# Audio tower on one Trainium2 core: sending each token's 1 / deviation through DRAM instead of through transposes, and moving one DCT ahead of the first gate

## The chip, the core and the metric

The kernel runs on one core of a Trainium2 chip, in float32 throughout. The metric is the time of one execution on the device, in microseconds (us). The time before is the median of three runs: 1388.79 us (1387.68 to 1390.09). The profiled execution took 1388.02 us, and its profile spans 1386.3 us.

The core has five engines that run their own instruction streams in order and wait for each other by semaphores: TensorE (PE; its weight loads are listed apart as PEld), VectorE (DVE), ScalarE (ACT), GpSimd (POOL) and SyncE (SP), which issues most DMA transfers.

## What is computed

There are 64 audio streams of 80000 samples. Each is cut into 157 frames of 512 samples, and a 512-point DCT turns each frame into a token `h` of 512 numbers. One layer follows, with an attention over the stream and a routed expert. Cut to what matters:

```
h = frames @ DCT.T                                   # 64 x 157 x 512
x = (h - mean(h)) / sqrt(var(h) + 1e-5)              # per token
key, query = tanh(x @ Wk + bk) * pi, tanh(x @ Wq + bq) * pi
V = x @ Wv + bv
total = sum over 4 sets of weight * Re(cumsum(e^(i key) V) * e^(-i query))
gate = sigmoid(x @ Wg + bg)
total = gate * total + (1 - gate) * pos_contribution
h = h + x + total / norm @ Wo + bo
x2 = layernorm(h);  e = argmax(softmax(mean(x2) @ Wg_ffn + bg_ffn))   # one expert per stream
h = h + score * (x2 @ We[e] + be[e])
```

The division by the deviation is what the change is about. The mean is taken out of the weights once, at the start of the program, so only one factor per token, 1 / deviation (`rstd`), has to reach the tokens before they are projected.

## The kernel before, in words

The 64 streams go in 16 groups of 4 (`NG`, `GB`). A group has 4 x 160 = 640 token slots, held as five tiles of 128 tokens (0 to 3 and `TAIL`). They stand in the order of `SLOT`, so that the first half of the slots (320, `HN`) is tile 0, tile 1 and half of the tail, and the second half is the rest of the tail and tiles 2 and 3.

A group's frames arrive as `xT`, 128 partitions x 4 x 640: samples on partitions, tokens along the free dimension. `fold_once` and `fold_twice` (lines 115 to 132) make the DCT cheaper by adding and subtracting mirrored samples in place. After that `xT` is both the operand of the DCT and, since the DCT is worked into the projection weights, the operand of all projections.

`embed` (line 241) does the DCT of one tile on PE into a PSUM buffer. `embed_statistics` (line 257) finishes it on DVE, takes its mean and variance there (lines 224 and 226), and lets POOL make `rstd` (lines 228 and 229), the shift (231) and `rstd` + 1 (267). `embed_res` (line 271) then reads the PSUM buffer on ACT (line 281) and writes the first part of the residual, which frees the buffer.

Here tokens lie on partitions, so `rstd` is one number per partition. In `xT` tokens lie along the free dimension, and there the factor must be the same in all partitions. `scale_all` (line 288) brings it there: six PE transposes (line 298) of `rstd`, repeated along the free dimension, fill a PSUM buffer, and two DVE multiplications (line 304), one for each half, scale `xT` in place.

All PSUM comes from one pool of four buffers of two banks each (line 83), taken in rotation by `psum()` and `bank()`. A buffer is taken again when all readers of its former content are through.

The order of the instructions on each engine is that of the program text: the schedule is written out by hand. From group 1 on, a group goes through `project_and_values`, `gate`, `experts_and_embedding` (the experts of the group before, the embedding of the next) and `attention`.

In `attention(g)` (line 1055), after the reading of the memory, the output projection is done as seven products (`output_product`, line 624), in the order 1, 2, 6, 7, 4, 5, 3. Product 7 is the one to follow:

- On DVE, product 7 is added to `u` (line 642).
- On POOL, three additions then take `u` into three quarters of the residual (line 630), `r22`, `r21` and `r12` in this order. They use `nc.gpsimd`, except in the last group.
- `scale_all(g + 1)` follows at once (line 1079).
- Product 4 is added into `r21` on DVE (line 657), product 5 into `r22` (line 647), then come the statistics of tiles 2 and 3 (`statistics2`), and the additions of products 5 and 3 into `r12`.
- `normal2(2)` makes the normalized tile 2 on ACT (line 677), after POOL has made its factor and shift.

`project_and_values(g + 1)` (line 960) begins on PE with the transposes of the normalized tail (line 690), the projection of keys and queries (line 524, on the scaled `xT`), and the transposes of normalized tile 2.

In the first group there is no such steady order. `first_values` ends with the DCT of tile 0 of group 1; `first_gate` (line 923) computes the gate of group 0 in four parts (`gate_part`, PE at line 560, ACT at 568) and between them does the rest of group 1's embedding, the scores, the additions of `bo` on POOL (line 286), and sums of the weights (`weights`, DVE at line 98).

Of the kernel before, what the change touches and what calls it, by code (L numbers as in the profile page):

```python
# [22 lines left out]
P = 128  # L23
# [30 lines left out]
def audio_tower(ctx: ExitStack, tc: tile.TileContext, a, out):  # L54
# [26 lines left out]
    p2 = pool("p2", 2)  # L81
    small = pool("small", 8)
    ps_mm = pool("ps_mm", 4, space=bass.MemoryType.PSUM)

    def load(name, shape, src=None):
        t = const.tile(shape, F32, name=name, tag=name)
# [3 lines left out]
    def psum():  # L90

        return ps_mm.tile([P, 2, 512], F32, tag="mm", name="mm")
# [31 lines left out]
    def fold_twice(g, m):  # L124

        if g < NG:
            ft, even = half(S[g]["xT"], m), S[g].pop(("even", m))
            add(ft[:, 2], even[:, 0], even[:, 1])
            sub(ft[:, 3], even[:, 0], even[:, 1])
            for n in range(2):  # L130
                to, by = ft[:, n], ft[:, 1 - n]
                nc.vector.scalar_tensor_tensor(to, by, lift[:, n : n + 1], to, ALU.mult, ALU.add)
# [85 lines left out]
        sub(raw, raw, ps.unsqueeze(1).to_broadcast([P, C, n]))  # L218


    def statistics(h):

        st = small.tile([P, 6], F32, tag="st", name="st")
        nc.vector.bn_stats(st, h)
        mv = small.tile([P, 2], F32, tag="mv", name="mv")
        nc.vector.bn_aggr(mv, st)  # L226
        rstd = small.tile([P, 1], F32, tag="rstd", name="rstd")
        nc.gpsimd.tensor_scalar(rstd, mv[:, 1:2], EPS, None, ALU.add)  # L228
        nc.gpsimd.tensor_tensor(rstd, rstd, power, ALU.pow)  # L229
        shift = small.tile([P, 1], F32, tag="shift", name="shift")  # L230
        nc.gpsimd.tensor_scalar(shift, mv[:, 0:1], rstd, -1.0, ALU.mult, ALU.mult)  # L231
        return rstd, shift
# [24 lines left out]
    def embed_statistics(g, n):  # L257
        s = S[g]
        h, odd = s.pop(("h", n))
        by_r = h.rearrange("p (j r) -> p r j", r=4)  # L260
        sines = p2.tile([P, P + 1], F32, tag="sines", name="sines")
        nc.scalar.copy(sines, odd[:, 1, : P + 1])
        add(by_r[:, 1, :], odd[:, 0, :P], sines[:, :P])
        sub(by_r[:, 3, :], odd[:, 0, 1 : P + 1], sines[:, 1 : P + 1])
        rstd, shift = statistics(h)
        rstd1 = small.tile([P, 1], F32, tag="rstd1", name="rstd1")
        nc.gpsimd.tensor_scalar(rstd1, rstd, 1.0, None, ALU.add)  # L267
        s["rstd", n] = rstd
        s["st", n] = h, shift, rstd1
# [14 lines left out]
    def add_bo(g, n):  # L284
        r = S[g]["res"][n]
        nc.gpsimd.tensor_tensor(r, r, bo, ALU.add)  # L286

    def scale_all(g):

        s = S[g]  # L290
        ps = psum()
        lo = 0

        for n in (0, 1, TAIL, TAIL, 2, 3):
            rows = slice(0, P) if n != TAIL else slice(0, HT) if lo < HN - 1 else slice(HT, P)
            m, at = divmod(lo, HN)
            w = rows.stop - rows.start
            nc.tensor.transpose(  # L298
                ps[:, m, at : at + w], s["rstd", n][rows].to_broadcast([w, P]), ident[rows, rows]
            )  # L300
            lo += w
        for m in range(2):
            x = half(s["xT"], m)
            nc.vector.tensor_tensor(x, x, ps[:, m, :HN].unsqueeze(1).to_broadcast([P, C, HN]), ALU.mult)


    def quarters(w):
# [230 lines left out]
    def phasors(g, of=(0, 1)):  # L538
        u = S[g]["u"]
        for n, to in ((0, kf), (1, qf)):  # L540
            if n not in of:
                continue
            for k in range(2):
                rows = slice(2 * F * k + F * n, 2 * F * k + F * (n + 1))
                to_k = to.rearrange("p s b t -> p (s b t)")[:, HN * k : HN * (k + 1)]
                nc.scalar.activation(to_k[F : 2 * F], u[rows, 0], AF.Sin, scale=PI)
                nc.scalar.activation(to_k[:F], u[rows, 1], AF.Sin, bias=quarter[rows], scale=-PI)
# [299 lines left out]
    def first_values():  # L847

        consts = constants()
        warm(12)  # L850
        made = [psum(), psum()]
        of = [ps[:, b, :] for ps in made for b in range(2)]
        for k in range(2):
            through_dct(raw_v, k, of[k], stop=False)
        total = add_up(raw_v, D, "x2T")
        for k in range(2, C):
            through_dct(raw_v, k, of[k], stop=False)
        fold_once(0, 0, nc.vector)
        fold_twice(0, 0)
        for k in range(C):  # L860
            less_mean(total, k, of[k])
            if k % 2:
                nc.scalar.copy(wv[:, k - 1 : k + 1], made[k // 2])
        embed(0, 0)
        embed(0, 1)
        embed_statistics(0, 0)
        embed_statistics(0, 1)
        embed_res(0, 0)
        embed_res(0, 1)
        value(0, 0)  # L870
        ps = psum()
        mean_kq, new_kq = ps[:, 0, : 2 * F], ps[:, 1, : C * 2 * F].rearrange("p (c n) -> p c n", c=C)
        means(add_up(raw_kq, 2 * F, "sum2"), mean_kq)
        centre(raw_kq, mean_kq, 2 * F)
        fold_once(0, 1, nc.vector)
        fold_twice(0, 1)
        value(0, 1)
        for k in range(C):
            through_dct(raw_kq, k, new_kq[:, k])
        nc.scalar.copy(wkq, new_kq)  # L880
        keep_value(0, 0)
        embed(0, 2)
        embed(0, 3)
        keep_value(0, 1)
        embed_statistics(0, 2)
        embed_statistics(0, 3)
        embed_res(0, 2)
        embed_res(0, 3)
        total = add_up(raw_g, D, "x2T", nc.gpsimd)
        value(0, 2)  # L890
        embed(0, TAIL)
        embed_statistics(0, TAIL)
        embed_res(0, TAIL)
        keep_value(0, 2)
        next(consts)
        value(0, 3)
        mean_g = bank()
        means(total, mean_g)
        centre(raw_g, mean_g, D)
        value(0, TAIL)  # L900
        keep_value(0, 3)
        keep_value(0, TAIL)
        scale_all(0)
        made = [psum(), psum()]
        for k in range(C):
            through_dct(raw_g, k, made[k // 2][:, k % 2])
        nc.scalar.copy(wg[:, :2], made[0])
        fold_once(1, 0)
        fold_twice(1, 0)
        fold_once(1, 1)  # L910
        project(0)
        nc.scalar.copy(wg[:, 2:], made[1])
        fold_phases(0)
        embed(1, 0)
        embed_statistics(1, 0)
        next(consts)
        phasors(0, (0,))
        embed_res(1, 0)
        phasors(0, (1,))
        next(consts)  # L920
        next(consts)

    def first_gate():

        made = chain(weight_sums(wv, t_v), weight_sums(wo, t_o))

        def weights():
            next(made)
            next(made)

        gate_part(0, 0)
        weigh()
        fold_twice(1, 1)
        weights()
        embed(1, 1)
        embed_statistics(1, 1)
        embed_res(1, 1)
        add_bo(0, 0)
        weights()
        gate_part(0, 1)  # L940
        scores(0)
        embed(1, 2)
        embed_statistics(1, 2)
        embed_res(1, 2)
        add_bo(0, 1)
        weights()
        gate_part(0, 2)
        weights()
        for n in (3, TAIL):
            embed(1, n)  # L950
            embed_statistics(1, n)
        for n in (3, TAIL):
            embed_res(1, n)
        gate_part(0, 3)
        for n in (2, 3, TAIL):
            add_bo(0, n)
        load_half(2, 0)
        load_half(2, 1)

    def project_and_values(g):  # L960

# [59 lines left out]
    def experts_and_embedding(g):  # L1021

        new = g + 1

        def embedded(n):
            embed_statistics(new, n)
            embed_res(new, n)

        add_bias(g - 1, TAIL)
        expert(g - 1, TAIL)  # L1030
        for n in range(3):
            embed(new, n)
            embed_statistics(new, n)
        add_bias(g - 1, 0)
        for n in range(3):
            embed_res(new, n)
        add_bv(g, 0)
        load_half(g + 2, 0)
        load_half(g + 2, 1)
        expert(g - 1, 0)  # L1040
        add_bias(g - 1, 1)
        add_bv(g, 1)
        expert(g - 1, 1)
        embed(new, 3)
        embed(new, TAIL)
        embed_statistics(new, 3)
        embed_statistics(new, TAIL)
        embed_res(new, 3)
        embed_res(new, TAIL)
        add_bias(g - 1, 2)  # L1050
        expert(g - 1, 2)
        add_bias(g - 1, 3)
        expert(g - 1, 3)

# [199 lines left out]
```

## Time and profile before

| | busy, us | share of the span | instructions |
|---|---|---|---|
| PE | 1376.4 | 99% | 10656 |
| PEld | 914.5 | 66% | 10656 |
| DVE | 1030.7 | 74% | 2076 |
| ACT | 402.9 | 29% | 690 |
| POOL | 604.3 | 44% | 858 |

The DMA engines moved 119.70 MB at a mean of 86 GB/s. Of the transfers, the frames (640 KB each) take a median of 4.6 us from issue to landing, and the result's pieces of 64 KB a median of 1.7 us.

The lines of the timeline read: start and duration in us, engine, line of the kernel, operation, tiles out<-in, partitions x elements out<-in, how many instructions in a row; in brackets the idle time before, and what ended it. A group of instructions starts where its first one starts. `mm` is a PSUM buffer. A lower-case q behind an engine's name is its sequencer.

### The profile page before, as it was taken

The numbers are of one execution on the slowest core, as the hardware profiler recorded it, in microseconds if no ns is written. First come the engines' busy times: TensorE is split into PE (matmuls) and PEld (weight loads), VectorE is DVE, ScalarE is ACT, GpSimd is POOL, SyncE is SP. The second block draws the span as 40 slices with busy tenths as digits, with TensorE's granted clock in tenths as the row PEclk, the third lists the DMA queues.
The fourth block names the chain that finished last, engine by engine and source line by source line (L and its number), as shares of the span: only waits on it lengthen the run. The fifth ranks groups of instructions, "written<-read, shape, count | busy, mean of one in ns | idle before, by whom it ended". The sixth has DMA issues, their size and how long they took to land.

```text
span 1386.3 us, 26936 instructions
## 1 busy us (share of the span) xinstructions
PE 1376.4 (99%) x10656; PEld 914.5 (66%) x10656; DVE 1030.7 (74%) x2076; ACT 402.9 (29%) x690; POOL 604.3 (44%) x858
## 2 busy tenths in 40 slices
PE   9999999999999999999999999999999999999998
PEld 5577575766758667575675757667586675766762
DVE  5768686777868778686776868778687777867674
ACT  2414242141422314242142422314223142421410
POOL 2453544525544254533535445255433545345314
PEclk9999999999999999999999999999999999999999
DMA  6013205032140323205032040322303232040306
GB/s 224 1 40 129 76 5 186 17 130 77 59 140 9 137 70 129 77 1 181 25 130 77 19 171 16 130 77 85 115 7 137 69 130 76 1 147 22 130 8 197
DMA packets 47293, 119.70 MB, mean 86 GB/s; under 512 B 9265, under 2 KB 26305, under 8 KB 39233
## 3 DMA queue, kind: packets, MB, share of 16 engines
q0 software_dynamic: 11456, 72.10, 13.5%
q1 hardware_dynamic: 35212, 45.26, 11.1%
q8 instruction: 84, 1.38, 0.4%
q10 hardware_dynamic: 500, 0.64, 0.2%
q14 instruction: 41, 0.33, 0.1%
HBM read 97.39 MB, written 20.58 MB: 85 GB/s over the span
## 4 chain that ended last, share of the span: by engine, by line
PE 97%; DVE 1%; DMA 1%; ACT 1%; issue 0%; POOL 0%; SPq 0%; DVEq 0%; POOLq 0%
PE mm L372 27%; PE mm L817 20%; PE mm L579 17%; PE mm L614 9%; PE mm L237 9%; PE mm L252 3%; PE mm L690 3%; PE mm L524 3%; PE mm L254 2%; PE mm L598 1%; PE mm L298 1%; PE mm L198 1%; PE mm L560 1%; DMA t_v<-in_we,rows 0%; DMA wv<-in_wv 0%; PE mm L709 0%
## 5 line engine op out<-in xcount | busy, mean ns | idle before, releaser
L228 POOL TENSOR_SCALAR rstd<-mv 128x1 f32<-128x1 f32 x160 | 44.6, 279 | 515.8 <-DVE mv L226 505.9
L817 PE MATMUL mm<-we,x2T 128*32 128x512 f32 x2400 | 267.4, 594 | 0.0
L817 PEld LDWEIGHTS mm<-we,x2T 128*32 128x32 f32 x2400 | 73.2, 110 | 161.3 <-issue 157.1
L99 DVE TENSOR_TENSOR gT<-mm,gT 128x128 f32<-128x128 f32 (+1 forms) x135 | 87.0, 673 | 82.6 <-PE mm L579 81.1
L622 DVE TENSOR_TENSOR gT<-mm,gT 128x320 f32<-128x320 f32 x256 | 116.8, 487 | 27.3 <-PE mm L614 22.9
L614 PE MATMUL mm<-att,v 32*128 32x256 f32 (+3 forms) x2048 | 123.6, 359 | 0.0
L614 PEld LDWEIGHTS mm<-att,v 32*128 32x128 f32 x2048 | 105.0, 185 | 22.3 <-issue 11.8
L589 ACT ACTIVATE gT<-gT,hbg 128x320 f32<-128x320 f32 x120 | 59.6, 554 | 168.6 <-DVE gT L99 168.6
L229 POOL TENSOR_TENSOR rstd<-rstd,power 128x1 f32<-128x1 f32 x160 | 98.1, 613 | 13.3
L828 DVE SCALAR_TENSOR_TENSOR res<-mm,gate,res 128x512 f32<-128x512 f32 x64 | 48.1, 751 | 68.3 <-PE mm L817 66.8
L677 ACT ACTIVATE x<-res,shift,rstd 128x512 f32<-128x512 f32 x64 | 52.1, 815 | 142.6 <-DVE res L99 101.0
L771 POOL DMA_INDIRECT we<-in_we,rows x60 | 62.0, 1034 | 71.4 <-DVE rows L767 57.7
L372 PE MATMUL mm<-t_o,sum 128*128 128x256 f32 x384 | 88.3, 379 | 0.4 <-DVE sum L98 0.4
L121 POOL TENSOR_TENSOR xT<-xT 128x640 f32<-128x640 f32 x30 | 46.7, 1557 | 91.6 <-DVE even L99 84.7
L286 POOL TENSOR_TENSOR res<-res,bo 128x512 f32<-128x512 f32 x64 | 85.6, 1366 | 0.0
L99 DVE TENSOR_TENSOR v<-mm,v 128x512 f32<-128x512 f32 x105 | 70.8, 686 | 18.8 <-PE mm L372 18.4
L372 PE MATMUL mm<-t_v,sum 128*128 128x256 f32 x360 | 82.7, 379 | 0.0
L281 ACT ACTIVATE res<-mm,shift,rstd 128x512 f32<-128x512 f32 x64 | 49.8, 778 | 103.9 <-POOL rstd L267 80.8
L372 PEld LDWEIGHTS mm<-t_o,sum 128*128 128x128 f32 x384 | 71.9, 190 | 11.7 <-PE mm L372 0.8
L231 POOL TENSOR_SCALAR shift<-mv,rstd 128x1 f32<-128x1 f32 x160 | 70.7, 442 | 16.5
L99 DVE TENSOR_TENSOR res<-mm,res 128x512 f32<-128x512 f32 x96 | 65.2, 685 | 15.0 <-ACT u L633 11.8
L630 POOL TENSOR_TENSOR res<-res,u 128x512 f32<-128x512 f32 x45 | 56.1, 1275 | 42.1 <-DVE u L99 42.1
(199 smaller groups left out, 2797.8 us busy)
## 6 DMA issues: line engine op xcount, KB each, us to landing
xT<-in_frames SPq DMA_DIRECT2D x32, 640.0 KB, 4.6
out<-res SPq DMA_DIRECT2D x236, 64.0 KB, 1.7
out<-res_t SPq DMA_DIRECT2D x62, 32.0 KB, 1.6
out<-res_t SPq DMA_DIRECT2D x62, 26.0 KB
wv<-in_wv SPq DMA_DIRECT2D x2, 512.0 KB, 5.5
wg<-in_wg SPq DMA_DIRECT2D x1, 1024.0 KB
wo<-in_wo SPq DMA_DIRECT2D x1, 1024.0 KB
we<-in_we,rows POOLq DMA_INDIRECT x60, 7.8
```

What stands on the lines that cost most here:

```text
L99: add = lambda *x: nc.vector.tensor_tensor(*x, ALU.add)
L229: nc.gpsimd.tensor_tensor(rstd, rstd, power, ALU.pow)
L231: nc.gpsimd.tensor_scalar(shift, mv[:, 0:1], rstd, -1.0, ALU.mult, ALU.mult)
L237: nc.tensor.matmul(ps, tile_of(x[:, c], n), w[:, c, :], start=(c == 0), stop=(c == C - 1))
L286: nc.gpsimd.tensor_tensor(r, r, bo, ALU.add)
L372: nc.tensor.matmul(ps[:, b, :], lhs[:, c, P * b : P * (b + 1)], w[:, c, :], start=(c == 0), stop=(c == 1))
L579: nc.tensor.matmul(ps[:, o, :HN], w[:, c, o * P : (o + 1) * P], rhs[:, c], start=(c == 0), stop=(c == 1))
L589: nc.scalar.activation(to, to, AF.Tanh, bias=hbg[:, c : c + 1], scale=0.5)
L614: nc.tensor.matmul(to, s["v", n][q, c * P : (c + 1) * P], by, start=(n == 3), stop=(n == TAIL))
L622: nc.vector.tensor_tensor(th, r[:, :, n], th, op)
L771: nc.gpsimd.indirect_dma_start(out=ws[b][:, n * k : n * (k + 1)], out_offset=None, in_=of, in_offset=bass.IndirectOffsetOnAxis(ap=rows[:, ...
L817: nc.tensor.matmul(ps[Q * i : Q * (i + 1), :], s["x2T"][:, c, i, Q * n : Q * (n + 1)], s["ws"][i][:, c, :], start=(c == 0), stop=(c == C - 1),
```

## The change

It has two parts.

**From group 1 on, `rstd` goes through DRAM.** `embed_statistics` writes it into a column of a tile `deviations`, 128 x 5. When all five are made, `keep_deviations` stores the tile to a row of 640 numbers in DRAM, in token order, and `spread_deviations` loads this row into all 128 partitions of a tile `scale` in SBUF. Both are issued from SP. `scale` shares its two buffers with `even`, the intermediate result of the folding. `scale_all` then has only the two multiplications, whose second operand is now in SBUF and no longer in PSUM. Group 0 keeps the transposes. In the steady order the store stands after the statistics of the tail in `experts_and_embedding`, the load after the expert of tile 2.

**In the first group the order changes.** The DCT of tile 1 of group 1 goes on PE ahead of `share` and the first gate part, its statistics ahead of the query phasors, and its `embed_res` behind them. One pair of weight sums moves behind gate part 1, and the others follow later.

```
-        rstd, shift = statistics(h)
+        if g == 0:
+            to = None
+        else:
+            if n == 0:
+                s["deviations"] = p2.tile([P, NM], F32, tag="deviations", name="deviations")
+            to = s["deviations"][:, SLOT[n] : SLOT[n] + 1]
+        rstd, shift = statistics(h, to)
...
+    def keep_deviations(g):
+
+        S[g]["row"] = row = dram.tile([NM, P], F32, tag="row", name="row")
+        nc.sync.dma_start(out=row.rearrange("s p -> p s"), in_=S[g]["deviations"])
+
+    def spread_deviations(g):
+
+        s = S[g]
+        s["scale"] = scale = p2.tile([P, 2, HN], F32, tag="even", name="scale")
+        row = s.pop("row").rearrange("s p -> (s p)")
+        nc.sync.dma_start(out=scale.rearrange("p m t -> p (m t)"), in_=row.partition_broadcast(P))
...
-        ps = psum()
...
+        if g == 0:
+            scale = psum()
...
+        else:
+            scale = s.pop("scale")
         for m in range(2):
             x = half(s["xT"], m)
-            nc.vector.tensor_tensor(x, x, ps[:, m, :HN].unsqueeze(1).to_broadcast([P, C, HN]), ALU.mult)
+            nc.vector.tensor_tensor(x, x, scale[:, m, :HN].unsqueeze(1).to_broadcast([P, C, HN]), ALU.mult)
...
         embed_statistics(1, 0)
+        embed(1, 1)
         next(consts)
         phasors(0, (0,))
         embed_res(1, 0)
-        phasors(0, (1,))
         next(consts)
         next(consts)
+        embed_statistics(1, 1)
+        phasors(0, (1,))
+        embed_res(1, 1)
...
         fold_twice(1, 1)
+        add_bo(0, 0)
+        gate_part(0, 1)
         weights()
-        embed(1, 1)
-        embed_statistics(1, 1)
-        embed_res(1, 1)
-        add_bo(0, 0)
-        weights()
-        gate_part(0, 1)
         scores(0)
         embed(1, 2)
         embed_statistics(1, 2)
         embed_res(1, 2)
         add_bo(0, 1)
         weights()
+        weights()
         gate_part(0, 2)
-        weights()
         for n in (3, TAIL):
             embed(1, n)
             embed_statistics(1, n)
+        keep_deviations(1)
         for n in (3, TAIL):
             embed_res(1, n)
+        weights()
         gate_part(0, 3)
...
+        spread_deviations(1)
...
         embed_statistics(new, TAIL)
+        keep_deviations(new)
         embed_res(new, 3)
         embed_res(new, TAIL)
         add_bias(g - 1, 2)
         expert(g - 1, 2)
+        spread_deviations(new)
```

More of the change, by code (lines that the diff above doesn't have):

```diff
@@ L83, in audio_tower @@
     ps_mm = pool("ps_mm", 4, space=bass.MemoryType.PSUM)
+    dram = pool("dram", 2, space=bass.MemoryType.DRAM)
     def load(name, shape, src=None):
@@ L218, in centre, with statistics @@
         sub(raw, raw, ps.unsqueeze(1).to_broadcast([P, C, n]))
-    def statistics(h):
+    def statistics(h, rstd=None):
         st = small.tile([P, 6], F32, tag="st", name="st")
@@ L226, in statistics @@
         nc.vector.bn_aggr(mv, st)
-        rstd = small.tile([P, 1], F32, tag="rstd", name="rstd")
+        if rstd is None:
+            rstd = small.tile([P, 1], F32, tag="rstd", name="rstd")
         nc.gpsimd.tensor_scalar(rstd, mv[:, 1:2], EPS, None, ALU.add)
@@ L286, in add_bo @@
         nc.gpsimd.tensor_tensor(r, r, bo, ALU.add)
+    def keep_deviations(g):
[6 more added lines that the diff above has]
+        nc.sync.dma_start(out=scale.rearrange("p m t -> p (m t)"), in_=row.partition_broadcast(P))
     def scale_all(g):
         s = S[g]
-        ps = psum()
[L292 to L301, printed above, removed]
+        if g == 0:
+            scale = psum()
+            lo = 0
+            for n in (0, 1, TAIL, TAIL, 2, 3):
+                rows = slice(0, P) if n != TAIL else slice(0, HT) if lo < HN - 1 else slice(HT, P)
+                m, at = divmod(lo, HN)
+                w = rows.stop - rows.start
+                nc.tensor.transpose(
+                    scale[:, m, at : at + w], s["rstd", n][rows].to_broadcast([w, P]), ident[rows, rows]
+                )
+                lo += w
+        else:
+            scale = s.pop("scale")
         for m in range(2):
             x = half(s["xT"], m)
-            nc.vector.tensor_tensor(x, x, ps[:, m, :HN].unsqueeze(1).to_broadcast([P, C, HN]), ALU.mult)
+            nc.vector.tensor_tensor(x, x, scale[:, m, :HN].unsqueeze(1).to_broadcast([P, C, HN]), ALU.mult)
     def quarters(w):
```

## The prediction, made before the changed kernel was run

> **What bounds the kernel now.** I read the page's busy times first, then the chain that ended last, then the timeline of one steady period (83.94 us; I take the one whose scaling stands at 685 us) and that of the first gate.
>
> ```profile
> PE 1376.4 (99%) x10656; PEld 914.5 (66%) x10656; DVE 1030.7 (74%) x2076; ACT 402.9 (29%) x690; POOL 604.3 (44%) x858
> PE 97%; DVE 1%; DMA 1%; ACT 1%; issue 0%; POOL 0%; SPq 0%; DVEq 0%; POOLq 0%
> ```
>
> PE is never idle in the steady part, so a removed PE instruction is worth its time, unless PE then has to wait for what used to arrive just ahead of it. PE's timeline from the transposes on, then those of DVE, POOL and ACT:
>
> ```profile
> 684.99 0.94 PE L298 MATMUL mm<-ident,rstd 128*128 128x128 f32 x6
> 685.77 1.89 PE L372 MATMUL mm<-t_o,gT 128*128 128x256 f32 x8
> ...
> 690.96 0.60 PE L690 MATMUL mm<-ident,x_t 128*128 128x128 f32 x4
> 691.49 2.38 PE L524 MATMUL mm<-xT,wkq 128*64 128x320 f32 x16
> 693.79 0.66 PE L690 MATMUL mm<-ident,x 128*128 128x128 f32 x4
> ```
>
> ```profile
> 685.19 0.69 DVE L99 TENSOR_TENSOR u<-mm,u 128x512 f32<-128x512 f32 x1 [0.44 <-PE mm L372]
> 685.97 2.89 DVE L304 TENSOR_TENSOR xT<-xT,mm 128x1280 f32<-128x1280 f32 x2
> 688.78 1.35 DVE L99 TENSOR_TENSOR res<-mm,res 128x512 f32<-128x512 f32 x2
> 690.16 0.69 DVE L224 BATCH_NORM_STATS2 st<-res 128x6 f32<-128x512 f32 x1
> ```
>
> ```profile
> 685.97 3.74 POOL L630 TENSOR_TENSOR res<-res,u 128x512 f32<-128x512 f32 x3 [2.81 <-DVE u L99]
> 691.16 0.22 POOL L228 TENSOR_SCALAR rstd<-mv 128x1 f32<-128x1 f32 x1 [1.44 <-DVE mv L226]
> ```
>
> ```profile
> 692.43 0.81 ACT L677 ACTIVATE x<-res,shift,rstd 128x512 f32<-128x512 f32 x1 [8.42 <-DVE res L99]
> ```
>
> The next matmuls follow the six transposes by 685.77 - 684.99 = 0.78 us: that is what they cost PE. Second, the margin behind them is small. Normalized tile 2 is ready at 692.43 + 0.81 = 693.24, and PE transposes it at 693.79: 0.55 us to spare. It comes out of a closed chain: DVE adds into `r21` from 688.78, then `r22`, statistics, POOL's factor and shift, ACT; 4.46 us from 688.78 to 693.24. Third, POOL's three additions and DVE's two multiplications begin at the same moment and do not disturb each other: 1.27 us and 1.48 us each, as fast as anywhere.
>
> That is because the multiplications have one operand in PSUM. With both operands in SBUF the same engines do disturb each other. First DVE begins and POOL follows 0.12 us later; then the reverse:
>
> ```profile
> 664.22 1.76 POOL L286 TENSOR_TENSOR res<-res,bo 128x512 f32<-128x512 f32 x1
> 664.10 0.74 DVE L811 SCALAR_TENSOR_TENSOR res<-be,gate,res 128x512 f32<-128x512 f32 x1
> ```
>
> ```profile
> 1305.21 2.36 POOL L439 TENSOR_TENSOR v<-v,bv 128x1024 f32<-128x1024 f32 x1
> 1305.73 2.36 DVE L600 TENSOR_TENSOR att<-att,share 128x480 f32<-128x480 f32 x1
> ```
>
> POOL's addition (1.26 us at its shortest) took 1.76 us: 0.50 us more, all but 0.12 of the 0.62 us that the DVE instruction still had to run. In the second case DVE's addition (0.66 us in the other periods) took 2.36 us and ended 0.52 us after POOL's. Whoever comes second waits for the whole instruction.
>
> The last view is the first gate, PE's timeline and the windows (columns: stretch, its length, busy us of PE, PEld, DVE, ACT and POOL, then PE's clock):
>
> ```profile
> 65.32 7.38 PE L560 MATMUL mm<-xT,wg 128*128 128x320 f32 x16 [2.94 <-ACT res L281]
> ```
>
> ```profile
> 60.80:64.20 3.40, 1.57 (x36) 1.33 (x24) 3.30 (x7) 0.00 (x0) 2.06 (x3) 1.00 0.00 0
> 64.20:71.00 6.80, 5.68 (x11) 3.72 (x12) 4.07 (x9) 2.00 (x4) 4.48 (x8) 0.50 0.00 0
> ```
>
> Gate part 2 waited 2.94 us for ACT to empty the PSUM buffer of tile 1's DCT, and the pause also cost half of PE's clock for 6.8 us: the part took 7.38 us where the others take 4.47.
>
> [...]
>
> **The change part by part.**
>
> *Transposes.* 15 x 6 removed, 15 x 0.78 = 11.7 us of PE. One PSUM buffer less is taken in each period, so the products behind it find theirs no later.
>
> *Store and load.* A store of 640 single numbers and a load of 128 x 2560 B = 328 KB. The last `rstd` is made at 663.7; at 0.6 us an issue, the store's landing after 1.7 to 6 us, four result stores between, then the load at 2 to 4.6 us (half of the frames' 640 KB would take less than 4.6), the row is in place by some 670 to 677, and DVE wants it at 685.9. On SP the store waits for POOL; behind it stand results of tile 2, made at 664.2; behind the load's wait, those of tile 3, made at 667.6. Nobody waits for these soon. Price: nothing, hidden under the last two experts and the memory reads (664 to 675).
>
> *The multiplications.* As long as before (an SBUF-only addition of 640 takes 0.82, one with PSUM 0.82), so 1.48 us each, but now in conflict with POOL's additions. Worked through for 685 us: DVE's first begins at 685.8 to 685.9, POOL's `r22` at 685.97 is stopped until 687.3 and ends at 688.4; DVE's second, stopped in turn, ends at 689.75; POOL's `r21` runs behind it and ends at 690.9. If POOL doesn't get in between, the multiplications end at 688.7, `r22` at 689.8, `r21` at 691.0: the same. The sum is 2 x 1.4 + 2 x 1.15 = 5.1 us from 685.9 either way. DVE's addition into `r21` needs it and starts at 691.0, not 688.78: 2.22 us late. Behind it in DVE's queue is all of the chain above, so tile 2 is ready at 693.24 + 2.22 = 695.46, and PE transposes it at 695.55 instead of 693.79: **+1.76 us a period**, though PE would have come 0.78 earlier. PE stands still in two places: before the key and query projection (its buffer is that of product 4, free at 691.0 + 0.69; PE arrives at 690.7: 1.0 us) and before tile 2's transposes (1.5 us). What follows (tile 3, tiles 0 and 1, the token sums) has 0.9 us and more to spare and moves along. No later part of the period has idle PE time to win it back. 15 x 1.76 = 26.4 us.
>
> *First gate.* With tile 1's DCT ahead, gate part 2 reuses the buffer of gate part 0, which ACT empties by about 61 us; PE wants it at 62.4. Part 3 wants tile 2's buffer at 69, free at 67 to 68. I expect no pause: -2.94 - (7.38 - 4.47) = -5.85, say **-5.8 us**.
>
> Sum: 1388.8 + 26.4 - 5.8 = 1409.4 us.
>
> **Rivals.**
> - *The multiplications don't hold POOL up* (a repeated operand might be read otherwise; no row before shows one from SBUF beside POOL). Then tile 2 is ready at 693.2 as before, PE gains 0.54 us of its 0.78 a period: 1388.8 - 15 x 0.54 - 5.8 = 1374.9 us, 1371.3 at best. For it: PE is at 99% and the transposes are gone. Against it: the four rows above.
> - *The pauses also cost clock.* [...]about 1425 us.
> - *The first gate keeps a pause elsewhere*, POOL's additions of `bo` now falling on DVE's folding: 1415 us.
>
> **How the numbers follow.** Chances: forecast 0.60, clock 0.18, first gate 0.05, not held up 0.15, something between that ends at no change 0.02. Predicted 1409.4. The forecast itself spans some 1398 to 1417 (1.2 to 2.2 us a period); with the clock rival's likelier part, up to 1438, the range holds about 8 in 10. Faster 0.15, same 0.02, slower 0.83.
>
> **What would show it.** POOL's L630 and DVE's multiplications stretched from 6.8 us of work side by side into one after the other; DVE's `r21` addition some 5.1 us after POOL is released, not 2.8; PE idle about 1.0 us before L524 and 1.5 us before the next L690; a period of 85.7 us; gate part 2 at 4.5 us without a pause. I am wrong if L630 stays at 1.27 us and the period falls below 83.9, or if the clock drops in the steady part.

## The result, and the profile after

| | median, us | lowest to highest | runs |
|---|---|---|---|
| before | 1388.24 | 1387.04 to 1390.09 | 4 |
| after | 1504.72 | 1499.96 to 1511.39 | 4 |

The ratio is 1.0841, 95% interval [1.0797, 1.0886]: 116.5 us slower, where I had forecast 21 us slower and a range that ended at 1438. The profiled execution of after spans 1498.2 us, before 1386.3: 111.9 us more. Line numbers of after are its own: the read of the memory is L637 (before L614), POOL's three additions L653 (L630), the multiplications L327 (L304), the key and query projection L547 (L524), the transposes of the normalized tiles L713 (L690).

The page's busy times and the chain that ended last:

```profile
PE 1409.2 (94%) x10566; PEld 943.2 (63%) x10566; DVE 1046.1 (70%) x2076; ACT 403.3 (27%) x690; POOL 638.7 (43%) x858
PE 85%; DVE 5%; POOL 5%; issue 4%; ACT 1%; another core or an unknown queue 0%; POOLq 0%
```

PE executes 90 instructions fewer, the transposes, and yet is busy for 32.8 us more; the other 79.1 us are idle time of PE (1498.2 - 1409.2 = 89.0, before 9.9). DVE and POOL have entered the chain with 5% each, which I expected, and "issue" with 4%, which I didn't; "issue" is time in which PE waited for nothing that the profile shows. PE's waits by line (in total, times, longest) divide the idle time:

```profile
PE mm L637 <- issue: 45.9, 26, 4.6
PE mm L713 <- ACT x L700: 20.2, 15, 1.4
PE mm L547 <- DVE res L100: 13.5, 15, 0.9
```

The second and third are the forecast conflict, once in each of 15 periods. The first, in the read of the memory, is new.

**The forecast part.** The timeline of one period, DVE, then POOL, then PE:

```profile
736.02 0.69 DVE L100 TENSOR_TENSOR u<-mm,u 128x512 f32<-128x512 f32 x1 [0.44 <-PE mm L395]
736.62 3.96 DVE L327 TENSOR_TENSOR xT<-xT,scale 128x1280 f32<-128x1280 f32 x2
741.74 1.29 DVE L100 TENSOR_TENSOR res<-mm,res 128x512 f32<-128x512 f32 x2 [1.16 <-POOL res L653]
```

```profile
736.79 6.15 POOL L653 TENSOR_TENSOR res<-res,u 128x512 f32<-128x512 f32 x3 [2.81 <-DVE u L100]
```

```profile
742.49 2.37 PE L547 MATMUL mm<-xT,wkq 128*64 128x320 f32 x16 [0.89 <-DVE res L100]
746.21 0.66 PE L713 MATMUL mm<-ident,x 128*128 128x128 f32 x4 [1.35 <-ACT x L700]
```

The two multiplications take 3.96 us instead of 2.89 and POOL's three additions 6.15 instead of 3.74; the addition into `r21` starts at 741.74, 5.12 us after the start of the multiplications. PE stands still 0.89 us before the projection (forecast 1.0) and 1.35 us before tile 2's transposes (forecast 1.5). The group rows of the page say the same of all periods: before, POOL's additions had a mean of 1275 ns.

```profile
L653 POOL TENSOR_TENSOR res<-res,u 128x512 f32<-128x512 f32 x45 | 92.3, 2076 | 42.1 <-DVE u L100 42.1
```

The first gate went as forecast too. Gate part 2 has no wait and no slow clock:

```profile
61.92 4.47 PE L583 MATMUL mm<-xT,wg 128*128 128x320 f32 x16
```

**The part that I had not forecast.** The read of one period, around the store of the 640 deviations. First SP, then PE, then DVE:

```profile
249.80 0.39 SPq L299 DMA_DIRECT2D row<-deviations  x1
250.29 1.88 SPq L858 DMA_DIRECT2D out<-res  x4
261.54 0.34 SPq L306 DMA_DIRECT2D scale<-row  x1
```

```profile
254.56 1.53 PE L637 MATMUL mm<-att,v 32*128 32x320 f32 x24
259.83 0.37 PE L637 MATMUL mm<-att,v 32*128 32x128 f32 x1 [3.74 <-issue]
261.15 0.89 PE L637 MATMUL mm<-att,v 32*128 32x128 f32 x4 [0.95 <-issue]
```

```profile
261.31 2.86 DVE L645 TENSOR_TENSOR gT<-mm,gT 128x320 f32<-128x320 f32 x6 [7.57 <-remote]
```

The store is issued at 249.80. The load of the row, which waits for its landing, starts at 261.54, 11.7 us later; over the periods it is 10.0 to 11.7 us. PE runs on until 256.1, stands until 261.2 but for one matmul at 259.83, and starts again about when the store lands. DVE, which has to add what PE has read, waits 7.57 us ("remote" stands where the profile names no releaser), almost up to the same moment, although PE's matmuls for it had ended at 254.74. The trace's semaphore events say where that time is: the updates of PE's semaphore by those matmuls are recorded at 261.28, 6.5 us after their ends, and in between POOL's own updates come on time (254.49, 255.72, 256.94). So PE was through with this work, but its word was held up, and with it DVE.

PE's own pause is not a wait for DVE's answer, though. The matmul at 259.83 and the weight load at 261.14, at which PE goes on, wait for no semaphore, and PE is at work at 261.15, before DVE begins at 261.31. In the period whose store is issued at 708.05 the two come apart: DVE got PE's word at 714.43 and began, and PE stood still afterwards all the same.

```profile
714.43 1.94 DVE L645 TENSOR_TENSOR gT<-mm,gT 128x320 f32<-128x320 f32 x4 [2.45 <-PE mm L637]
```

```profile
717.53 0.46 PE L637 MATMUL mm<-att,v_t 32*128 32x64 f32 x1 [1.82 <-issue]
719.38 0.80 PE L637 MATMUL mm<-att,v_t 32*128 32x64 f32 x4 [1.38 <-issue]
```

So two things go with the store: PE's word comes late (in this period it was still 5 us ahead of the load of the row at 719.70, so it doesn't always come with the landing), and PE itself stands still without waiting for anything that is on record.

The DMA view of the stretch from 249.5 to 262.5 us (40 slices of 0.325 us: the engines' busy share in tenths, then GB/s):

```profile
DMA  1001764663900000000000000000000000000002
GB/s 25 0 0 1 7 133 107 164 170 82 151 0 0 0 0 0 0 0 0 0 0 0 0 0 0 0 0 0 0 0 0 0 0 0 0 0 0 0 0 50
```

Up to 253.1 us packets are on record, then for 9 us no byte. And the pause costs clock as well. The windows of the same stretch (columns: stretch, its length, busy us of PE, PEld, DVE, ACT and POOL, PE's clock, DMA share, GB/s):

```profile
249.00:255.50 6.50, 6.50 (x92) 3.35 (x88) 2.22 (x4) 1.14 (x2) 6.31 (x8) 1.00 0.49 42
255.50:261.50 6.00, 1.31 (x21) 0.82 (x15) 0.19 (x1) 0.00 (x0) 1.43 (x2) 0.81 0.02 0
261.50:267.00 5.50, 5.50 (x67) 4.95 (x70) 3.90 (x9) 0.00 (x0) 0.00 (x0) 0.58 0.42 110
```

PE works 1.31 of 6.00 us, and what it then catches up on runs at a clock of 0.58. Over the span PE's clock is at half for 75 us, before for 8. By my estimate the 67 us more cost 33 us of work; that is the larger part of why PE is busy for longer with less to do, though not all (32.8 us more, and 11.7 of transposes gone). The clock halved in 13 of the 15 periods, for 3.4 to 10.2 us each. A period lasts 88.7 to 94.6 us instead of 83.94.

### The profile page after: what moved, and what is told of

Its sections match the earlier page's. It is cut to its first block, busy times and chain, and to the rows that moved or that the text cites. A ratio compares the mean times of both kernels' runs of the same rounds, so it can differ in the third digit from the quotient of the medians.

```text
span 1498.2 us, 26759 instructions
## 1 busy us (share of the span) xinstructions
PE 1409.2 (94%) x10566; PEld 943.2 (63%) x10566; DVE 1046.1 (70%) x2076; ACT 403.3 (27%) x690; POOL 638.7 (43%) x858
## 2 busy tenths in 40 slices
DMA packets 59292, 124.66 MB, mean 83 GB/s; under 512 B 19344, under 2 KB 36384, under 8 KB 51232
## 3 DMA queue, kind: packets, MB, share of 16 engines
q8 instruction: 84, 1.38, 0.4%
## 4 chain that ended last, share of the span: by engine, by line
PE 85%; DVE 5%; POOL 5%; issue 4%; ACT 1%; another core or an unknown queue 0%; POOLq 0%
PE mm L395 20%; PE mm L840 19%; PE mm L602 15%; PE mm L637 11%; PE mm L239 8%; POOL res L653 5%; PE mm L254 3%; PE mm L256 2%; PE mm L713 2%; DVE res L100 2%; DVE st L225 1%; PE mm L583 1%; PE mm L621 1%; ACT x L700 1%; PE mm L199 1%
## 5 line engine op out<-in xcount | busy, mean ns | idle before, releaser
L637 PE MATMUL mm<-att,v 32*128 32x192 f32 (+3 forms) x2048 | 161.0, 411 | 41.4 <-issue 40.5
L637 PEld LDWEIGHTS mm<-att,v 32*128 32x128 f32 x2048 | 133.5, 216 | 72.2 <-issue 62.5
L230 POOL TENSOR_SCALAR rstd<-mv 128x1 f32<-128x1 f32 x85 | 20.7, 243 | 331.5 <-DVE mv L227 328.6
L230 POOL TENSOR_SCALAR deviations<-mv 128x1 f32<-128x1 f32 x75 | 25.5, 341 | 260.4 <-DVE mv L227 255.0
L653 POOL TENSOR_TENSOR res<-res,u 128x512 f32<-128x512 f32 x45 | 92.3, 2076 | 42.1 <-DVE u L100 42.1
L656 ACT COPY u<-mm 128x512 f32<-128x512 f32 x16 | 9.4, 587 | 267.7 <-PE mm L395 267.7
```

Source lines behind the costliest of these rows:

```text
L637: nc.tensor.matmul(to, s["v", n][q, c * P : (c + 1) * P], by, start=(n == 3), stop=(n == TAIL))
L653: more = lambda to, x: (nc.vector if last else nc.gpsimd).tensor_tensor(to, to, x, ALU.add)
```

## The experiments

After the result I had two theories of the surplus of some 95 us: the store of single numbers itself, or the two pauses of the conflict, by way of the clock (the rival that I had given 0.18). The runs first take the change apart, then the store, then look for a form of it that pays. Except where it is said, nothing of the computation is left out or changed.

### Each part alone

**The first gate alone**, before with the second part of the change only:

```
@@ first_values
         embed_statistics(1, 0)
+        embed(1, 1)
         next(consts)
...
+        embed_statistics(1, 1)
+        phasors(0, (1,))
+        embed_res(1, 1)
```

> Only the second part of the change: the new order of the first group, with the transposes kept. My forecast's step for it: gate part 2 no longer waits 2.94 us and runs at full clock, 5.8 us less than before, 1382.4 us. Rival (a pause moves elsewhere in the first gate): 1386 to 1389 us. If this part has a share in the 116 us lost: above 1395 us.

Measured: 1382.73 us, beside it before 1386.82; ratio 0.9972 [0.9962, 0.9981], so 4.1 us, where I forecast 5.8. The pause is gone, all of its 2.94 us. The rest of my 5.8 was what 6.8 us at half the clock had cost in before. In the profiles of kernels below that keep this pause the half clock behind it lasted 0, 3.4 or 6.8 us: the pause is the same each time, its price in clock is not. I had taken one execution's for the rule.

**The store alone**, before with the deviations stored as in the change, nobody reading them, and the transposes kept (POOL writes them into `deviations` as in the change; those lines and the first group's call are left out here):

```
+    def keep_deviations(g):
+
+        S[g]["row"] = row = dram.tile([NM, P], F32, tag="row", name="row")
+        nc.sync.dma_start(out=row.rearrange("s p -> p s"), in_=S[g]["deviations"])
...
         embed_statistics(new, TAIL)
+        keep_deviations(new)
```

> Before, plus only the store of the deviations to DRAM in 640 single numbers, at the change's place; nothing is loaded, the transposes and the multiplications from PSUM stay. Theory A (the store itself stops PE): PE stands still in the memory read for some 3 us a period with nothing shown as the cause, until the store has landed some 12 us after its issue, and the clock drops there: 45.9 + 37.4 us as in the changed kernel, so about 1470 us. Theory B (the load, or the conflict of DVE and POOL shifting everything, stops PE): within 3 us of before, 1388 to 1391 us.

Measured: 1479.35 us, ratio 1.0677 [1.0659, 1.0695]: 92.5 us for a transfer of 2.5 KB that nobody waits for. PE's waits (the read is L627 here):

```profile
PE mm L627 <- issue: 42.8, 36, 3.5
```

It is the same wait as in after, half the clock for 80 us included, and the multiplications still take their factors from PSUM, so the change's conflict of DVE and POOL is not there. So the surplus belongs to the store.

### What about the store

**In 128 pieces.** The same 640 numbers from the same tile, in the order in which they stand in it, five side by side from each partition:

```
-        S[g]["row"] = row = dram.tile([NM, P], F32, tag="row", name="row")
-        nc.sync.dma_start(out=row.rearrange("s p -> p s"), in_=S[g]["deviations"])
+        S[g]["row"] = row = dram.tile([P, NM], F32, tag="row", name="row")
+        nc.sync.dma_start(out=row, in_=S[g]["deviations"])
```

> As the store-only kernel, but the row lies in DRAM as the tile does, so that the store is 128 pieces of 20 B. Theory A1 (the number of single writes matters): landed within some 3 us, no pause of PE, 1388 to 1391 us. Theory A2 (any store of small pieces at this place stops PE): well above, 1400 us or more.

Measured: 1386.52 us, ratio 0.9997 [0.9988, 1.0005], a period of 83.94 us, no pause in the read. Free.

**640 single numbers, 512 B apart.** As many writes of 4 B as in the change, but each into its own 512 B:

```
-        S[g]["row"] = row = dram.tile([P, NM], F32, tag="row", name="row")
-        nc.sync.dma_start(out=row, in_=S[g]["deviations"])
+        S[g]["row"] = row = dram.tile([P, NM, P], F32, tag="row", name="row")
+        nc.sync.dma_start(out=row[:, :, 0], in_=S[g]["deviations"])
```

> As the store-only kernel (before plus a store of 640 single numbers, nothing loaded), but each number goes to a row of 512 B of its own in DRAM. Theory C (the writes get into each other's way since five rows of 512 B take all 640 of them, 18 ns each): the store lands in a few us and PE is not stopped, below 1400 us. Theory D (640 write requests take their 12 us wherever they go): as the store-only kernel, 1470 to 1485 us.

Measured: 1386.32 us, ratio 0.9995 [0.9987, 1.0004]. Free as well. So it is neither the number of writes nor their smallness; it is that many of them write side by side.

**64 B apart:**

```
-        S[g]["row"] = row = dram.tile([P, NM, P], F32, tag="row", name="row")
+        S[g]["row"] = row = dram.tile([P, NM, 16], F32, tag="row", name="row")
```

> The kernel before with the store of 640 single numbers alone, each number 64 B from the next (free when 512 B apart, 1479 when side by side in five rows of 512 B). Nothing of the computation is left out. If what the single writes share is a piece of 64 B or less: no pause, 1387. If it is the row of 512 B: eight writers a row instead of 128, so a hold of up to 12 us at the same 18 ns a number, 1479; or, if only writers of one row that are near in time collide, something between.

Measured: 1386.66 us, ratio 0.9999 [0.999, 1.0007]. Free: eight single writes in the same 512 B cost nothing when they are 64 B apart. That they share 512 B is thus not enough. Whether it is the distance that helps, or that only eight instead of 128 share the 512 B, this run doesn't separate. The semaphore events of the traces also give the landings of these stores: 2.2 to 3.5 us after the issue with 512 B between the numbers, 2.3 to 3.7 with 64 B.

**Single numbers read.** Before, with the store in 128 pieces, and a load of 640 single numbers out of what it wrote, into a tile that nobody reads:

```
+    def back_deviations(g):
+
+        back = p2.tile([P, NM], F32, tag="back", name="back")
+        row = S[g].pop("row").rearrange("p s -> (p s)").rearrange("(s p) -> p s", p=P)
+        nc.sync.dma_start(out=back, in_=row)
```

> The kernel before, with the deviations stored in 128 pieces of 20 B (which cost nothing in the run of that name) and then loaded again as 640 single numbers out of five rows of 512 B, into a tile that nobody reads. Nothing of the computation is left out. Theory 'single writes that share a row': [...]no pause: 1387, period 83.94. Theory 'single numbers, written or read': 640 reads of 4 B collide as the writes did, about 12 us from issue to landing, PE halted: some 1440 to 1480.

Measured: 1387.15 us, ratio 1.0001 [0.9992, 1.001]. Reads side by side are free. The run also times an undisturbed store of these numbers, from its issue to the load that waits for it, 1.44 us here and 1.4 to 2.4 over the periods:

```profile
662.05 0.34 SPq L299 DMA_DIRECT2D row<-deviations  x1
663.49 0.39 SPq L306 DMA_DIRECT2D back<-row  x1
```

**A fifth of the writes.** Single numbers side by side again, but only the 128 of the first tile, into one row of 512 B, and a load behind them to show the landing:

```
+        S[g]["row"] = row = dram.tile([1, P], F32, tag="row", name="row")
+        nc.sync.dma_start(out=row.rearrange("s p -> p s"), in_=S[g]["deviations"][:, :1])
...
+        back = p2.tile([1, P], F32, tag="back", name="back")
+        nc.sync.dma_start(out=back, in_=S[g].pop("row"))
```

> The kernel before with a store of single numbers side by side again, but of the first tile's 128 deviations alone (one row of 512 B instead of five), and a load of that row behind it, which shows when the store has landed. Nothing of the computation is left out. Theory 'the writes go one after the other, some 18 ns each': the load starts 1.7 + 2.3 = 4 us after the store's issue; the memory read is 5 to 6 us ahead of what the hold touches, so no pause: 1387, period 83.94. Theory 'one after the other only inside a row, five rows at a time': 128 writes take as long as 640 did, the load starts some 12 us after the issue and PE halts as before: about 1479.

Measured: 1388.63 us, ratio 1.0004 [0.9997, 1.0011]. SP's timeline:

```profile
238.36 0.38 SPq L299 DMA_DIRECT2D row<-deviations  x1
246.40 0.23 SPq L304 DMA_DIRECT2D back<-row  x1
```

8.0 us here, 7.8 to 9.5 over the periods: between what the two theories had expected (4 and 12), so neither holds. A fifth of the writes needs some 70% of the time. The same number of writes as 20 B pieces (the store of the run before) needs 1.4 to 2.4 us, so the landing time isn't set by the count of writes but mostly by how close together they lie: 16 in each 64 B here and in the change, 3 or 4 with 20 B pieces, one in the run 64 B apart (which landed in 2.3 to 3.7 us). PE doesn't pause, and its signals are on time here, those of 5 to 8 us after the issue too (within 0.3 us of the matmuls' ends). So a store that lands late doesn't by itself hold up PE's signals; with 640 numbers it did, with 128 it didn't, and why is not shown.

**Another place.** The full store, of the current group's deviations (long made), ahead of the experts, to see whether PE stops there too:

```
         add_bias(g - 1, TAIL)
+        keep_deviations(g)
         expert(g - 1, TAIL)
```

> As the store-only kernel (640 single numbers into five rows, nothing loaded), but it stores the deviations of the group that is being worked on, long made, ahead of the experts (14 times), where PE issues some 18 instructions a us for over 14 us; in the memory read it issues some 37. Theory E (PE runs out of instructions, which come by DMA transfers of 16 KB and stand behind the store): its stock lasts longer there and PE is hardly stopped, below 1410 us. Theory F (the store stops PE whatever it does): a pause and a dropped clock of the same kind some 6 us behind the issue, 1450 us or more.

Measured: 1420.54 us, ratio 1.0224 [1.0199, 1.0249]. The test didn't go where I meant it to. SP has its own queue of result stores ahead of this one and reached it only late, 2.8 us into the read; SP and then PE:

```profile
941.86 1.29 SPq L299 DMA_DIRECT2D row<-deviations  x1
```

```profile
939.04 1.80 PE L627 MATMUL mm<-att,v 32*128 32x320 f32 x32
948.69 2.74 PE L239 MATMUL mm<-wo,gT 128*128 128x512 f32 x6
954.70 1.18 PE L239 MATMUL mm<-wo,gT 128*128 128x512 f32 x2 [3.27 <-DVE gT L635]
```

```profile
953.63 1.02 DVE L635 TENSOR_TENSOR gT<-mm,gT 128x320 f32<-128x320 f32 x2 [5.78 <-remote]
```

Still it tells something. PE finishes the whole read here and begins the output projection; what comes late is again PE's word: the updates by matmuls that ended at 946.93, 948.85 and 951.43 are all recorded between 953.61 and 953.77, 11.8 us after the store's issue, and DVE stands still until then. In this run PE stops mostly where it needs DVE's answer:

```profile
PE mm L239 <- DVE gT L635: 16.6, 9, 3.3
PE mm L239 <- issue: 0.9, 1, 0.9
```

The pauses without a visible reason are almost absent, the others are shorter than the 42.8 us of the store-only run, and the clock dropped in 3 of the periods only; the same store costs 33 us here (1420.54 - 1387.23) instead of 92.

The theory that PE runs out of instructions finds no support in the trace of after. In 11 of the 14 periods in which PE stands still in the read, no transfer of the kind "instruction" is on record during the longest pause, so PE went on without one. This run alone would fit that theory, since the store lands here while PE is in the products, where it issues fewer instructions (6 matmuls in 2.74 us at 948.69, 32 in 1.80 in the read at 939.04); what stops PE in the read stays open.

### The change without its store's cost

**The row in 128 pieces.** After, with the store of 20 B pieces and the row loaded as it stands; the multiplications then read the factors with a step of 20 B:

```
+            by = scale.rearrange("p m t -> p (m t)").rearrange("p (q s) -> p s q", s=NM)
+            for m in range(2):
+                x = s["xT"][:, 2 * m : 2 * m + 2].rearrange("p c (s q) -> p c s q", q=P)
+                nc.vector.tensor_tensor(x, x, by.unsqueeze(1).to_broadcast([P, 2, NM, P]), ALU.mult)
```

> The changed kernel with the row kept in the order of the tile (store of 128 pieces of 20 B), the load as before in 128 x 2560 B, and the multiplications reading it with a step of five numbers, two blocks of the samples at a time. If the 640 single writes are what I missed, the rest of my forecast should come out: POOL and DVE one after the other, PE idle 0.9 and 1.35 us a period as in the changed kernel, no pause in the memory read: 1405 to 1412 us. If the load also stops PE: above 1440 us. If the strided reading is slow on DVE, the multiplications are longer than 1.5 us and PE's second pause is longer by that.

Measured: 1440.43 us, ratio 1.0385 [1.0368, 1.0402], and I had expected 1405 to 1412. The pause in the read is gone; what I missed is that the multiplications became longer. DVE's multiplications and POOL's additions (times of one in ns: lowest, median, highest), and PE's waits:

```profile
L333 DVE TENSOR_TENSOR xT<-xT,scale x30: 2472/2508/3569, 92.2 to 1325.1; 128x1280 f32<-128x1280 f32 x30
```

```profile
L659 POOL TENSOR_TENSOR res<-res,u x45: 1256/3441/5869, 92.4 to 1330.0; 128x512 f32<-128x512 f32 x45
```

```profile
PE mm L553 <- DVE res L100: 44.2, 15, 3.1
PE mm L719 <- ACT x L706: 8.0, 6, 1.3
```

The multiplication takes 2.47 us at its shortest instead of 1.48, 1.0 us more on 1280 elements. (This run also takes `xT` in other blocks, two of the four at a time, so the step is not the only difference.) And the longer multiplications cost POOL the same again: in the period whose multiplications start at 707.54 us the two take 5.96 us instead of 3.96, and POOL's three additions 8.15 instead of 6.15. PE now waits 2.9 us before the projection in each period, and this pause does cost clock, in 9 of them.

**The row in order.** So ACT, which is idle then, first copies the row into token order, and DVE multiplies as in the change:

```
+    def order_deviations(g):
+
+        s = S[g]
+        s["scale"] = scale = p2.tile([P, 2, HN], F32, tag="even", name="scale")
+        nc.scalar.copy(
+            scale.rearrange("p m t -> p (m t)").rearrange("p (s q) -> p s q", q=P),
+            s.pop("spread").rearrange("p m t -> p (m t)").rearrange("p (q s) -> p s q", s=NM),
+        )
```

> The changed kernel with the store in 128 pieces of 20 B, the load in 128 x 2560 B, and a copy on ScalarE that puts the spread row into token order in SBUF ahead of the memory reads; the multiplications are those of the changed kernel, at their place, with no steps in their operands. This leaves only the conflict of DVE and POOL and the first gate: PE idle 0.9 and 1.35 us a period, period 85.5 us, no pause in the memory read and no drop of the clock: 1405 to 1411 us. If the load also costs, above 1420 us.

Measured: 1407.42 us, ratio 1.0145 [1.013, 1.0161]; 20.2 us above before (1387.23). PE's waits:

```profile
PE mm L722 <- ACT x L709: 20.2, 15, 1.4
PE mm L556 <- DVE res L100: 13.4, 15, 0.9
```

This is the change as I had costed it: the two pauses in each period, a period of 85.54 us, no half clock in the steady part. The load of the row, which the store-only run lacks, is in this run and adds nothing. The two pauses alone cost no clock; that rival falls.

### Where the multiplications can go

**On GpSimd, ahead of the output products.** In after POOL is idle for 17 us between the additions of `bo` and the factor of the tail, and the row is there early in that stretch once its store is quick:

```
-            nc.vector.tensor_tensor(x, x, scale[...], ALU.mult)
+            (nc.vector if g == 0 else nc.gpsimd).tensor_tensor(x, x, scale[...], ALU.mult)
...
+        if ahead:
+            scale_all(g + 1)
         for i in (1, 2, 6, 7, 4, 5, 3):
...
-            elif i == 7 and ahead:
-                scale_all(g + 1)
```

> As the row-in-order kernel, but the two multiplications are done by POOL ahead of the output products, where it is idle for some 10 us in the kernel before; about 3.2 us each. If the conflict is what costs the row-in-order kernel its time, DVE's addition into r21 waits for POOL's alone, the period is 83.94 - 0.78 = 83.2 us and the whole some 1371 to 1373 us, faster than before and than the first-gate part alone. If POOL's multiplications last until its three additions are due, PE's pauses stay: above 1385 us.

Measured: 1376.97 us, ratio 0.9932 [0.9918, 0.9945], faster than before and than the first gate alone. The steady period is 83.16 us: 83.94 minus the 0.78 us of the transposes, all of it. It is 4 us above the range that I expected, and the first group has most of that. Its read is short, the row comes late, and POOL's multiplications run into DVE's sums over the tokens (POOL, DVE, PE):

```profile
83.02 6.20 POOL L336 TENSOR_TENSOR xT<-xT,scale 128x1280 f32<-128x1280 f32 x2
```

```profile
83.98 2.50 DVE L100 TENSOR_TENSOR sum<-gT 128x512 f32<-128x512 f32 x1
86.51 3.26 DVE L99 TENSOR_TENSOR sum<-sum,gT 128x512 f32<-128x512 f32 x1
```

```profile
89.91 1.97 PE L404 MATMUL mm<-t_o,sum 128*128 128x256 f32 x8 [2.13 <-DVE sum L99]
```

A sum that takes 0.68 us elsewhere takes 2.50 and 3.26, and PE waits 2.13 + 0.76 + 0.27 = 3.16 us in all.

**The second group by transposes.** So group 1, whose row is wanted in the first group's short read, is scaled as before:

```
-        if g == 0:
+        if g < 2:
             scale = psum()
...
-        keep_deviations(1)
...
-        spread_deviations(1)
```

> The kernel with the row in 128 pieces, the copy on ACT and the multiplications on GpSimd, but with the second group (the one whose row is wanted in the first group's read, which is short) scaled by transposes and on DVE as before, so 14 rows instead of 15. In the run before this, that one place cost PE 2.13 + 0.76 + 0.27 = 3.16 us; six transposes cost 0.78. Expected: 1377.0 - 3.16 + 0.78 = 1374.6, 1373 to 1376; the steady period stays at 83.16. If the steady part held a cost too that I overlooked, it stays at 1376 or above.

Measured: 1372.95 us (1372.4 to 1373.33), ratio 0.9897 [0.988, 0.9913]. This version beats both kernels: 14.0 us less than before, 132 less than after. POOL's multiplications and its three additions of the same period, and the chain:

```profile
661.08 5.77 POOL L336 TENSOR_TENSOR xT<-xT,scale 128x1280 f32<-128x1280 f32 x2 [0.27 <-ACT scale L312]
675.88 3.72 POOL L662 TENSOR_TENSOR res<-res,u 128x512 f32<-128x512 f32 x3 [2.80 <-DVE u L100]
```

```profile
PE 97%; DMA 1%; DVE 1%; SPq 0%; issue 0%; POOL 0%; DVEq 0%; POOLq 0%
```

The multiplications take twice as long on POOL as on DVE and nobody minds; the additions are back at 3.72 us, and PE has the chain to itself.

## Why the prediction was wrong

The direction was right, the size was not: 1409.4 forecast, 1504.72 measured, outside the range. The runs price each step of the sum:

| step | forecast, us | measured, us | from |
|---|---|---|---|
| first gate | -5.8 | -4.1 | 1382.73 - 1386.82 |
| transposes away, multiplications in conflict (+1.76 a period, the 0.78 of the transposes included) | +26.4 | +24.3 | 1407.42 - 1387.23 + 4.1 |
| store and load | 0 | +92.5 | 1479.35 - 1386.82 |
| sum | +20.6 | +112.7 | after - before: +116.5 |

- **The failed step is "Store and load ... Price: nothing, hidden under the last two experts and the memory reads".** It has two faults. The landing was bounded at "1.7 to 6 us" from stores whose pieces were whole rows, and I let the 640 single numbers pass as the same kind of thing; it took 10.0 to 11.7. And I asked only who waits for the data. Nobody does, as I wrote, but while the store was landing PE's signals to DVE came late, by 6.5 us in the period shown, and PE stood still where it waited for nothing on record, for 42.8 us in the store-only run, and lost clock on top: 92.5 us instead of nothing. The layout shows in the count of packets: after has 19344 under 512 B, the version with 128 pieces 11664, so 7680 = 15 x 512 fewer. But the count isn't the cost: the store-only run has 19104 of them and the one with the numbers 512 B apart 19105, and that one was free (1386.32 us).
- **The multiplications were right.** 1.76 us a period forecast, 85.54 - 83.94 = 1.60 measured in the run with the row in order; the pauses 1.0 and 1.5 forecast, 0.89 and 1.35 measured. The rule that I had drawn from four rows of before (a second DVE operand in SBUF, and whoever comes second waits for the whole instruction) held for a repeated operand too: of the two multiplications of a period one takes 2.56 us instead of 1.48, of POOL's three additions two take 2.44 and 2.52 instead of 1.27. So "not held up" falls.
- **The first gate** lost its pause. Of the 5.8 us, 2.9 were clock, and the clock's loss behind that pause differs from one execution to the next (0, 3.4 or 6.8 us at half).
- **"The pauses also cost clock"** falls as I wrote it, and its 1425 us was my estimate, not shown by a trace: pauses of 0.89 and 1.35 us, which end 3.7 us apart, never halved the clock in 15 periods. Elsewhere a pause went with a loss of clock: the one of 2.9 us in 9 of 15 periods, the store's in 13 of 15.
- "The first gate keeps a pause elsewhere" falls: no wait stands there in after.

What stays open: by which way a store of single numbers holds up PE's semaphore updates, and what stops PE itself. That the store's layout decides is shown by the runs with the same numbers stored otherwise; the way is not. Each execution here has its span and its clock on record, so whether the recording of PE's many instructions has a part in its pauses is untested too. The time passes after the transfers themselves: in the run that stores at another place the packets of 4 B were all through 1.4 us after the issue in 12 of 14 periods, and the store had landed only some 7 us later or more. That writes side by side take turns is an inference of mine from five runs, not shown. If 16 writers of one 64 B piece took turns, each would need (8.0 - 1.4) / 16 = 0.41 us with 128 numbers but (11.5 - 1.4) / 16 = 0.63 with 640, and 3 or 4 would show with 20 B pieces, which landed in 1.4 us; so the picture is not complete.

## What to carry to other kernels

A transfer that nobody waits for is not free because of that (92.5 us here): look at how its writes lie in DRAM, and don't scatter single numbers side by side; store the tile as it stands (1386.52 us, free) and put it in order afterwards, on an engine that has time (1.38 us of ACT in each period). When an operand moves from PSUM to SBUF, see what GpSimd does at that moment (its three additions took 6.15 us here instead of 3.74), and if the work can be placed, put it on GpSimd itself in a stretch where DVE has no instruction with two SBUF inputs (beside POOL's multiplications its sums of 0.68 us took 2.50 and 3.26). A step priced at nothing deserves a range of its own, from the nearest row that really has its shape.

## What the runs showed of the hardware that I had not expected

- Single 4 B writes side by side in DRAM, from 128 partitions: 640 in five rows of 512 B land 10.0 to 11.7 us after the issue, 128 in one row 7.8 to 9.5, 128 pieces of 20 B 1.4 to 2.4. 640 single writes 64 B or 512 B apart, and 640 single reads side by side, cost the kernel nothing that could be measured (1386.66, 1386.32 and 1387.15 us; before, beside them, 1386.97, 1387.23 and 1386.97). So by these runs it is not the size of the writes alone that costs.
- During such a store of 640 numbers PE's semaphore updates were recorded 6.5 us (in another run 6.7 us) after the matmuls' ends, while POOL's came on time, and PE stood still for up to 4.6 us where it waited for nothing on record: 92 us in 15 periods for 2.5 KB each. With 128 numbers, which also took some 8 us to land, neither was seen.
- A DVE multiplication whose second SBUF operand is read with a step of 20 B took 2.47 us for 128 x 1280 numbers at its shortest (with `xT` taken in other blocks, too), 1.48 with the numbers side by side; ACT's copy that put 128 x 640 of them in order took 1.38 us.
